# Where the blend is multiplied in: the trace products of three batches, and the division of the scores, in a fused four-layer kernel

## The chip, the cores and the metric

One Trainium2 chip, one of its cores. The metric is the device time of one launch in microseconds (us), median of the runs shown.

## The reference, cut to what matters

A batch of 16 sequences x of 256 tokens and 256 channels goes through four layers, each with a residual. The change touches the first two.

```python
# layer 0: 16 decaying traces of a gated input
h1 = gelu(x @ Wn1.T + bn1)
mod = 0.5 + sigmoid(h1 @ Wn2.T + bn2)                 # (b, t, 16)
traces = [ema(gated * mod[..., d, None], tau[d]) for d in range(16)]
blend_w = softmax(blend, axis=0)                      # (16, channels)
temporal = einsum('dbtc,dc->btc', traces, blend_w)
gate = sigmoid(temporal @ Wtemp.T + btemp)
...
# layer 1: pooling with masked softmax
p = softmax(where(mask, scores[:, None, :], -1e30), -1)
pooled = (p @ hidden) / cnt[..., None]
...
# layer 2: 8 experts and a shared one (256 -> 1024 -> 256, Silu), each with weights of its own
# layer 3: 256 -> 1024 (Gelu) -> 256, a quarter of the last weight chosen per batch
```

Here ema is the recurrence h = alpha * h + input along the tokens. Since it is linear, the blend, which is a number for each trace d and channel c, may be multiplied into the input of the trace instead of into its result: the kernel feeds gated * mod[d] * blend[d, c].

## The kernel before, in words

Channels lie on the 128 partitions, in two halves (c = 0, 1), tokens in the columns; a tile of one batch is [128, 2, 256]. Weights and activations that go into TensorE are split into a rounded high part and the rest (`rnd` on line 88, `low` on line 95), and each product is three matmuls (`mm3`, lines 101 to 103).

For each batch b, `traces` (line 247) makes the gated input, the modulation and the 16 traces, and `pooled` (line 392) makes the rest of layer 0 and the pooling. Both are generators that yield after each step. The matmul units of layer 2 (`l2_unit`, line 620: up, gate, Silu, product, split, down) and layer 3 work on pairs of batches. The driver below line 820 walks a plan of units and runs steps of `traces` and `pooled` between them, at a rate (`pace`) such that a pair's batches are ready when its units come. The units of a pair wait until `pooled` of its second batch is done: batch 0 runs alone for five experts, then pair (0, 1), and then pair (2, 3), with two pairs at a time from there. The tile scheduler afterwards orders the instructions of each engine by its own estimates, so that an order is fixed when the program is built; each engine works through its queue in order.

What the change and the steps of the prediction touch:

- Line 287 to 295: md holds 0.5 + sigmoid for 16 traces on 48 partitions. For batches 1 to 15 it is stored to a DRAM tile mdd (line 295), from which rows are loaded back, repeated on all 128 partitions.
- Lines 351 to 354: for each pair of traces (d, d+1) one load of two rows of 256 into mod, a tile [128, 2, 256] with two buffers (tag "mod", `bufs=2`); eight loads per batch on SyncE's queue.
- Lines 358 to 361: bt = ga * bl * mod, in two `scalar_tensor_tensor` of 256 columns, one for each half c, because the blend bl[:, c, d] is a number per partition and differs between the halves. ga (gp in the profile) lies in PSUM for batches 1 to 15.
- Lines 362 to 367: two scans (the recurrence) into tr, and GpSimd adds tr to the sum ta.
- Batch 0 (`fast`) has another way, lines 325 to 348: mod comes from a matmul, ScalarE scales it by bl while it copies it out (line 335), and one product of 512 columns is left (line 338).
- Lines 474 to 485: the scores of the pooling: masked minimum, exponential with its sum on ScalarE (line 477), sums times counts and reciprocal on VectorE, and then sc times that number, in two `tensor_scalar` of 256 columns on VectorE (line 485); the result is transposed on TensorE (line 493, ppt).
- Lines 549 to 556: each weight chunk of an expert is loaded raw (two buffers), rounded on ScalarE (line 88) and its rest taken on VectorE, or on GpSimd for some (line 95).

Of the kernel before, what the change touches and what calls it, by code (L numbers as in the profile page):

```python
# [8 lines left out]
F32 = mybir.dt.float32  # L9
F32R = mybir.dt.float32r  # L10
I32 = mybir.dt.int32
AF = mybir.ActivationFunctionType
ALU = mybir.AluOpType
# [4 lines left out]
S = 256  # L18
P = 128
# [9 lines left out]
STORE = 2  # L29
LAG = 2  # L30
BOOST = 400
HOLD = 3
STEPS = {"traces": 21, "pooled": 10}
FIRST = 13
# [10 lines left out]
def fused_kernel(  # L45
# [20 lines left out]
    nc = tc.nc  # L66
    V, G, A, PE = nc.vector, nc.gpsimd, nc.scalar, nc.tensor
# [3 lines left out]
    l0 = ctx.enter_context(tc.tile_pool(name="l0", bufs=1))  # L71
# [68 lines left out]
    bl = const([P, 2, ND], F32, "bl", blend)  # L140
# [106 lines left out]
    def traces(b, fast):  # L247

        xr = xin_tiles.pop(b)
        xh, xl = hl(f"x_{b}", "hA")  # L250
        rnd("v" if fast else "a", xh, xr)
        low("v" if fast else "g", xl, xr, xh)
        cx = ft("ta", f"ctx{b}")
        for c in range(2):
            last_of["cx"] = V.tensor_tensor_scan(
                cx[:, c], decay[:, ND : ND + 1].to_broadcast([P, S]), xr[:, c], 0.0, ALU.mult, ALU.add
            )
        yield
        if fast:
            split_small(O_N1, "v")  # L260
        ch, cl = hl(f"c_{b}", "hA")
        rnd("a", ch, cx)
        low("v", cl, cx, ch)

        ph = ps_l.tile([P, 512], F32, tag="ps", name=f"ph{b}")
        for k in range(2):
            o = O_N1 + k * P
            mm3(ph[:, :S], W(0, o, P), W(1, o, P), xh[:, k], xl[:, k], k == 0, k == 1)
        if fast:
            with tc.issue_after(last_of["cx"].ins):  # L270
                split_small(O_G, "v")
                split_small(O_G + 512, "v")

                V.tensor_copy(coef[:, :, NE], sgt)
                V.tensor_scalar(sgt, sgt, -1.0, 1.0, ALU.mult, ALU.add)
                V.tensor_tensor(coef[:, :, 0:NE], gat, sgt.unsqueeze(2).to_broadcast([P, NB, NE]), ALU.mult)
        hg = l0.tile([P, S], F32, tag="hg", name=f"hg{b}")
        A.activation(hg, ph[:, :S], AF.Gelu, bias=vec[:, V_BN1 : V_BN1 + 1])
        hs = l0.tile([P, S], F32R, tag="hs", name=f"hs{b}")
        rnd("a", hs, hg)  # L280
        low("v", hs[64:], hg[64:], hs[64:])
        yield
        pm = ps_l.tile([P, 512], F32, tag="ps", name=f"pm{b}")
        PE.matmul(pm[:48, :S], n2[:, 0], hs, start=True, stop=False)
        PE.matmul(pm[:48, :S], n2[:, 1], hs, start=False, stop=True)
        md = l0.tile([48, S], F32, tag="md", name=f"md{b}")
        A.activation(md, pm[:48, :S], AF.Tanh, bias=hb[:48, V_BN2 : V_BN2 + 1], scale=0.5)
        V.tensor_scalar(md, md, 0.5, 1.0, ALU.mult, ALU.add)
        if fast:
            ms = l0.tile([48, S], F32R, tag="ths", name=f"ms{b}")  # L290
            rnd("v", ms, md)
            low("v", ms[32:], md[32:], ms[32:])
        else:
            mdd = dram.tile([1, ND, S], F32, tag="mdd", name=f"mdd{b}")
            nc.sync.dma_start(mdd[0], md[0:ND])
        yield
        pg = banks(fast, f"pg{b}")

        ga = ft("ga", f"ga{b}") if fast else ps_a.tile([P, 2, S], F32, tag="ga", name=f"gp{b}")
        for m in range(2):  # L300
            for k in range(4):
                o = O_G + k * S + m * P
                xa, xb_ = (xh[:, k], xl[:, k]) if k < 2 else (ch[:, k - 2], cl[:, k - 2])
                mm3(pg(m), W(0, o, P), W(1, o, P), xa, xb_, k == 0, k == 3)
        for m in range(2):
            A.activation(ga[:, m], pg(m), AF.Tanh, bias=hb[:, V_BG + m : V_BG + m + 1], scale=0.5)
        for c in halves(fast):
            V.scalar_tensor_tensor(ga[:, c], ga[:, c], 1.0, xr[:, c], ALU.add, ALU.mult)
        yield
        sm = ft("sm", f"sm{b}")  # L310

        def soma():
            pso = ps_l.tile([P, 2, S], F32, tag="ps", name=f"pso{b}")
            for m in range(2):
                for k in range(2):
                    o = O_SO + k * S + m * P
                    mm3(pso[:, m], W(0, o, P), W(1, o, P), xh[:, k], xl[:, k], k == 0, k == 1)
            for m in range(2):
                A.activation(sm[:, m], pso[:, m], AF.Gelu, bias=vec[:, V_BSO + m : V_BSO + m + 1])

        if fast:
            split_small(O_SO, "g")
            split_small(O_TE, "g")

            tacc = ps_y.tile([P, 2, S], F32, tag="y0", name=f"ta{b}")
            for d in range(ND):
                if d % 2 == 0:
                    pb = ps_gu.tile([P, 2, S], F32, tag="gu", name=f"pb{b}_{d}")
                    for i in range(2):
                        PE.matmul(  # L330
                            pb[:, i], sel[:, d + i : d + i + 1].to_broadcast([48, P]), ms, start=True, stop=True
                        )
                mod = l0.tile([P, 2, S], F32, tag="mod", name=f"mod{b}_{d}", bufs=2)
                for c in range(2):
                    last_of["a"] = A.activation(mod[:, c], pb[:, d % 2], AF.Copy, scale=bl[:, c, d : d + 1])
                bt = ft("bt", f"bt{b}_{d}", 3)
                e = "g" if d else "v"
                last_of[e] = (V if e == "v" else G).tensor_tensor(bt, ga, mod, ALU.mult)
                tr = ft("tr", f"tr{b}_{d}", 3)
                for c in range(2):  # L340
                    V.tensor_tensor_scan(
                        tr[:, c], decay[:, d : d + 1].to_broadcast([P, S]), bt[:, c], 0.0, ALU.mult, ALU.add
                    )
                PE.matmul(tacc, ident, tr, start=d == 0, stop=d == ND - 1)
                if d == 5:
                    soma()
                if d % 2:
                    yield
        else:
            tacc = ft("ta", f"ta{b}")  # L350
            for d in range(ND):
                if d % 2 == 0:
                    mod = l0.tile([P, 2, S], F32, tag="mod", name=f"mod{b}_{d}", bufs=2)
                    nc.sync.dma_start(mod, mdd[0, d : d + 2].partition_broadcast(P))
                bt = ft("bt", f"bt{b}_{d}", 3)
                tr = tacc if d == 0 else ft("tr", f"tr{b}_{d}", 3)
                with tc.issue_after(last_of[0].ins) if b == 1 and "h" not in last_of else nullcontext():
                    for c in range(2):
                        V.scalar_tensor_tensor(
                            bt[:, c], ga[:, c], bl[:, c, d : d + 1], mod[:, d % 2], ALU.mult, ALU.mult  # L360
                        )
                for c in range(2):
                    V.tensor_tensor_scan(  # L363
                        tr[:, c], decay[:, d : d + 1].to_broadcast([P, S]), bt[:, c], 0.0, ALU.mult, ALU.add
                    )
                if d:
                    G.tensor_tensor(tacc, tacc, tr, ALU.add)  # L367
                if d == 5:
                    soma()
                yield  # L370
        th, tl = hl(f"t_{b}", "hA")
        for c in halves(fast):
            rnd("a", th[:, c], tacc[:, c])
            low("v", tl[:, c], tacc[:, c], th[:, c])
        xt = xt_tiles.pop(b)
        G.tensor_tensor(xt, xt, bet.unsqueeze(1).to_broadcast([P, 2, S]), ALU.add)
        held[b] = xt, sm, th, tl
        yield
# [13 lines left out]
    def pooled(b, fast):  # L392
# [77 lines left out]
        sc = ft("sc", f"sc{b}")  # L470
        mx = l0.tile([P, 2], F32, tag="mx", name=f"mx{b}")
        sums = l0.tile([P, 2], F32, tag="sums", name=f"sums{b}")
# [8 lines left out]
        for j in halves(fast):  # L481
            V.tensor_tensor(sums[:, j], sums[:, j], cntb[:, b, j], ALU.mult)
            V.reciprocal(sums[:, j], sums[:, j])
            for i in range(j.start, j.stop):
                V.tensor_scalar(sc[:, i], sc[:, i], sums[:, i : i + 1], None, ALU.mult)
        vh, vl = hl(f"v_{b}", "hB")
        rnd("a", vh, x1)
        low("g", vl, x1, vh)
# [248 lines left out]

    def prefetch(n, boost=BOOST):
        while n > 0 and nxt[0] < len(order):
# [101 lines left out]
    for i, item in enumerate(plan):  # L841
        kind, args, _, done = item[:4]
# [130 lines left out]
```

## Time and profile before

| what | us |
|---|---|
| median of 3 runs (lowest, highest) | 2857.16 (2855.82, 2858.89) |
| profiled execution: its time, its span | 2854.52, 2852.3 |
| TensorE matmul busy | 2781.6 (98%) |
| VectorE busy | 1442.2 (51%) |
| ScalarE busy | 1239.2 (43%) |
| GpSimd busy | 1295.4 (45%) |
| L359, the products bt, all batches | 480 x, 207.2 busy, 475 ns mean |
| L363, the scans of tr | 450 x, 285.1 busy, 672 ns mean |
| L367, GpSimd's adds into ta | 225 x, 308.4 busy, 1371 ns mean |
| L354, loads of mod | 120 x, 256 KB each, 3.5 us median to landing |

A profile is one execution. A row of its groups names the line, the engine, the operation, the tile written and the tiles read, the shape and the count; then the busy time and the mean length of one; then how long the engine had been idle just before, and whom it waited for. "L88", "L95" and "L101" to "L103" are lines of helpers that many places call, so there the tiles' names tell the place. The timeline lists an engine's instructions by start. Neighbours on an engine overlap by some 0.08 us in it, so what one costs the queue is read from start to start. A table of stages gives each engine's busy time in chosen stretches of the span.

### The profile page before, as it was taken

To read this page: it belongs to the slowest core of one execution; us is meant where nothing else is said; L and a number is where in the kernel's file an instruction comes from. 1 tells how busy PE (TensorE), PEld (TensorE's weight loads), DVE (VectorE), ACT (ScalarE), POOL (GpSimd) and SP (SyncE) were. 2 spreads that over 40 slices of the span, in tenths; PEclk is the share of its full clock that TensorE was granted. 3 is DMA by queue.
4 is the path that set the end of the run, shared out by engine and by line. 5 is a ranking of instruction groups with operands and counts; after the bars stand their busy time and mean duration, and the time that the engine had idled before them with its cause. 6 is when DMAs were issued, how large, how long until landed. Compare 5 with 4: busy or idle time off the path is not lost. (4 is left out here: it accounts for less than half of the span.)

```text
span 2852.3 us, 36958 instructions
## 1 busy us (share of the span) xinstructions
PE 2781.6 (98%) x13632; PEld 2339.8 (82%) x13632; DVE 1442.2 (51%) x2661; ACT 1239.2 (43%) x2054; POOL 1295.4 (45%) x984
## 2 busy tenths in 40 slices
PE   6889889999999999999999999999999999999999
PEld 4887778888888888888888888888888888888887
DVE  7978866665665454444544445444444542222222
ACT  5565544456444533435334443344433453233433
POOL 4755544544645453543534445344454443333333
PEclk8999999999999999999999999999999999999999
DMA  3444546547443532323433143332523242222552
GB/s 106 132 144 137 162 149 217 176 144 244 149 159 120 172 123 100 118 80 92 173 105 125 40 167 117 107 118 66 181 100 110 93 159 98 89 89 76 189 196 86
DMA packets 114694, 371.24 MB, mean 130 GB/s; under 512 B 12642, under 2 KB 30930, under 8 KB 114514
## 3 DMA queue, kind: packets, MB, share of 16 engines
q1 hardware_dynamic: 113650, 368.74, 39.0%
q8 instruction: 108, 1.77, 0.3%
q14 instruction: 72, 0.59, 0.1%
q10 hardware_dynamic: 864, 0.14, 0.0%
HBM read 304.62 MB, written 64.21 MB: 129 GB/s over the span
## 5 line engine op out<-in xcount | busy, mean ns | idle before, releaser
L95 POOL TENSOR_TENSOR hh<-h,hh 128x512 fp32r<-128x512 f32 x640 | 848.4, 1326 | 1327.1 <-ACT hh L88 1307.4
L608 DVE TENSOR_TENSOR h<-h,pu 128x512 f32<-128x512 f32 x576 | 393.9, 684 | 939.6 <-PE pu L103 818.1
L88 ACT ACTIVATE hh<-h 128x512 fp32r<-128x512 f32 x640 | 403.5, 631 | 932.6 <-DVE h L608 912.4
L101 PE MATMUL pg<-x,w_e 128*128 128x512 f32 (+1 forms) x1232 | 467.3, 379 | 12.7 <-ACT x L88 5.4
L607 ACT ACTIVATE h<-pg 128x512 f32<-128x512 f32 x576 | 342.9, 595 | 306.6 <-PE pg L103 228.5
L101 PE MATMUL pu<-x,w_e 128*128 128x512 f32 (+1 forms) x1232 | 465.4, 378 | 6.5 <-ACT h L607 3.7
L103 PE MATMUL pg<-x,w_e 128*128 128x512 f32 (+1 forms) x1232 | 465.7, 378 | 4.2 <-DVE w_e L95 3.4
L102 PE MATMUL y<-hh,w_e 128*128 128x512 f32 (+1 forms) x1232 | 464.4, 377 | 3.2 <-POOL hh L95 3.2
L102 PE MATMUL pg<-x,w_e 128*128 128x512 f32 (+1 forms) x1232 | 465.3, 378 | 0.0
L103 PE MATMUL pu<-x,w_e 128*128 128x512 f32 (+1 forms) x1232 | 463.8, 376 | 0.0
L102 PE MATMUL pu<-x,w_e 128*128 128x512 f32 (+1 forms) x1232 | 463.6, 376 | 0.0
L103 PE MATMUL y<-hh,w_e 128*128 128x512 f32 (+1 forms) x1232 | 463.5, 377 | 0.0
L101 PE MATMUL y<-hh,w_e 128*128 128x512 f32 (+1 forms) x1232 | 415.6, 377 | 1.0 <-DVE acc L655 0.8
L367 POOL TENSOR_TENSOR ta<-ta,tr 128x512 f32<-128x512 f32 x225 | 308.4, 1371 | 67.6 <-DVE tr L363 53.9
L363 DVE TENSOR_TENSOR_SCAN tr<-decay,bt 128x256 f32<-128x256 f32 x450 | 285.1, 672 | 0.0
L101 PEld LDWEIGHTS pg<-x,w_e 128*128 128x128 f32 x1232 | 232.5, 189 | 56.4 <-ACT w_e L88 6.4
L101 PEld LDWEIGHTS pu<-x,w_e 128*128 128x128 f32 x1232 | 232.1, 188 | 50.5 <-ACT h L607 5.8
L103 PEld LDWEIGHTS pg<-x,w_e 128*128 128x128 f32 x1232 | 232.7, 189 | 47.8 <-DVE w_e L95 5.2
L102 PEld LDWEIGHTS y<-hh,w_e 128*128 128x128 f32 x1232 | 233.0, 189 | 47.0 <-POOL hh L95 5.5
L101 PEld LDWEIGHTS y<-hh,w_e 128*128 128x128 f32 x1232 | 231.5, 189 | 44.8 <-ACT hh L88 1.3
L103 PEld LDWEIGHTS y<-hh,w_e 128*128 128x128 f32 x1232 | 233.0, 189 | 41.7
L103 PEld LDWEIGHTS pu<-x,w_e 128*128 128x128 f32 x1232 | 232.3, 189 | 41.9
(294 smaller groups left out, 3267.5 us busy)
## 6 DMA issues: line engine op xcount, KB each, us to landing
w_e<-keep_e SPq DMA_DIRECT2D x216, 768.0 KB, 4.4
raw_e<-in_wexp_dram SPq DMA_DIRECT2D x144, 384.0 KB, 4.5
keep_e<-w_e SPq DMA_DIRECT2D x72, 768.0 KB, 4.2
mod<-mdd SPq DMA_DIRECT2D x120, 256.0 KB, 3.5
w_f<-keep_f SPq DMA_DIRECT2D x56, 384.0 KB, 3.6
raw_c<-in_comb_dram SPq DMA_DIRECT2D x32, 260.0 KB, 2.8
xr<-in_xT_dram SPq DMA_DIRECT2D x16, 256.0 KB, 3.1
xt<-in_x_dram SPq DMA_DIRECT2D x16, 256.0 KB, 2.7
```

What stands on the lines that cost most here:

```text
L88: last_of["ca"] = A.activation(out_, in_, AF.Copy)
L95: i = (V if e == "v" else G).tensor_tensor(out_, in_, h.bitcast(F32), ALU.subtract)
L101: PE.matmul(o, wh, xh, start=start, stop=False, **kw)
L102: PE.matmul(o, wh, xl, start=False, stop=False, **kw)
L103: last_of["pe"] = PE.matmul(o, wl, xh, start=False, stop=stop, **kw)
L363: V.tensor_tensor_scan(tr[:, c], decay[:, d : d + 1].to_broadcast([P, S]), bt[:, c], 0.0, ALU.mult, ALU.add)
L367: G.tensor_tensor(tacc, tacc, tr, ALU.add)
L607: A.activation(h, ps_g, AF.Silu)
L608: last_of["h"] = V.tensor_tensor(h, h, ps_u, ALU.mult)
```

## The change

For b below `LEAN` = 4 (with the other way of batch 0: batches 1, 2 and 3) each trace has a mod tile of its own. The load repeats one row into both halves, on all partitions; ScalarE multiplies each half in place by its blend; and VectorE makes one product of 512 columns. Batches 4 to 15 keep their products. The number of mod buffers stays two. For all batches but the first, ScalarE instead of VectorE multiplies the scores by the reciprocal.

```diff
+LEAN = 4
...
             for d in range(ND):
-                if d % 2 == 0:
+                if b < LEAN:
+                    mod = l0.tile([P, 2, S], F32, tag="mod", name=f"mod{b}_{d}", bufs=2)
+                    row = mdd[0, d : d + 1].partition_broadcast(P)
+                    nc.sync.dma_start(mod, row.to_broadcast([P, 2, S]))
+                    for c in range(2):
+                        A.activation(mod[:, c], mod[:, c], AF.Copy, scale=bl[:, c, d : d + 1])
+                elif d % 2 == 0:
                     mod = l0.tile([P, 2, S], F32, tag="mod", name=f"mod{b}_{d}", bufs=2)
                     nc.sync.dma_start(mod, mdd[0, d : d + 2].partition_broadcast(P))
...
-                    for c in range(2):
+                    if b < LEAN:
+                        V.tensor_tensor(bt, ga, mod, ALU.mult)
+                    for c in range(2 if b >= LEAN else 0):
                         V.scalar_tensor_tensor(
                             bt[:, c], ga[:, c], bl[:, c, d : d + 1], mod[:, d % 2], ALU.mult, ALU.mult
                         )
...
             for i in range(j.start, j.stop):
-                V.tensor_scalar(sc[:, i], sc[:, i], sums[:, i : i + 1], None, ALU.mult)
+                if fast:
+                    V.tensor_scalar(sc[:, i], sc[:, i], sums[:, i : i + 1], None, ALU.mult)
+                else:
+                    A.activation(sc[:, i], sc[:, i], AF.Copy, scale=sums[:, i : i + 1])
```

## The prediction

> **What bounds the kernel now.** I read the page's busy shares first: TensorE (PE) is busy for 98% of the span, so over most of the kernel nothing but fewer or better-fed matmuls counts. Then the table of stages, because the change touches only batches 1 to 3 in its larger part and a share over the whole span hides them. Columns: stretch in us, its length, busy us (instructions) of PE, weight loads, VectorE (DVE), ScalarE (ACT), GpSimd (POOL), then granted clock, DMA share, GB/s.
>
> ```profile
> 76.00:126.00 50.00, 44.90 (x341) 42.76 (x339) 49.45 (x87) 24.54 (x37) 42.03 (x28) 0.97 0.46 143
> 181.00:235.00 54.00, 50.09 (x258) 41.89 (x257) 53.29 (x91) 27.97 (x42) 40.22 (x28) 0.97 0.43 129
> 268.00:322.00 54.00, 45.35 (x196) 34.44 (x195) 53.40 (x97) 23.64 (x38) 35.73 (x26) 0.97 0.36 111
> 322.00:380.00 58.00, 58.00 (x346) 51.53 (x345) 40.18 (x65) 36.72 (x64) 25.80 (x20) 1.00 0.69 227
> 380.00:396.00 16.00, 9.96 (x58) 9.01 (x57) 5.86 (x18) 4.51 (x10) 0.00 (x0) 0.79 0.17 58
> 600.00:2800.00 2200.00, 2197.68 (x10365) 1843.28 (x10364) 973.08 (x1833) 901.78 (x1492) 948.04 (x732) 1.00 0.37 124
> ```
>
> The first three stretches are the trace stages of batches 1, 2 and 3. VectorE is busy for 49.45 of 50, 53.29 of 54 and 53.40 of 54 us: it is the bound there, and PE has gaps of 5, 4 and 9 us. From 322 to 380 and from 600 on PE has none, so an engine relieved there is worth nothing. At 380 to 396 PE is nearly idle: it waits for the end of batch 3's pooled steps, because the matmul units of the pair (2, 3) can't start before. Everything up to that point decides when the saturated rest begins.
>
> Next VectorE's timeline in batch 1's stage (start us, us, engine, line, operation, tiles, count); no row has an idle time before it:
>
> ```profile
> 78.03 1.26 DVE L363 TENSOR_TENSOR_SCAN ta<-decay,bt 128x256 f32<-128x256 f32 x2
> 79.21 0.66 DVE L608 TENSOR_TENSOR h<-h,pu 128x512 f32<-128x512 f32 x1
> 79.79 1.65 DVE L359 SCALAR_TENSOR_TENSOR bt<-gp,bl,mod 128x256 f32<-128x256 f32 x4
> 81.36 0.95 DVE L95 TENSOR_TENSOR w_e<-raw_e,w_e 128x768 fp32r<-128x768 f32 x1
> 82.23 2.43 DVE L363 TENSOR_TENSOR_SCAN tr<-decay,bt 128x256 f32<-128x256 f32 x4
> ```
>
> Read it by starts, since neighbours overlap: four L359 products take 81.36 − 79.79 = 1.57, so 0.78 us for one trace's two; one 128x512 product with a PSUM operand (L608) takes 79.79 − 79.21 = 0.58 us. Last the groups that price the rest:
>
> ```profile
> L335 ACT ACTIVATE mod<-pb,bl 128x256 f32<-128x256 f32 x32 | 13.3, 472 | 5.2 <-POOL bt L338 5.1
> L485 DVE TENSOR_SCALAR sc<-sc,sums 128x256 f32<-128x256 f32 x32 | 14.1, 479 | 0.5
> ```
>
> and, from the view of the tile mod up to 330 us, how long its loads take:
>
> ```profile
> DMA to landing us min/median/max: 3.0/3.4/4.8
> ```
>
> [...] The new product reads gp from PSUM and mod from SBUF, so I price it as L608.
>
> **The change, part by part.** *Products.* 3 batches x 16 traces: 96 L359 go, 48 products of 512 columns come. 0.78 − 0.58 = 0.20 us each, 48 x 0.20 = 9.6 us, all in stretches where VectorE has no idle time. This is the ceiling. (By durations instead of starts: 40.4 us of L359 in the three stretches, less 48 x 0.66, is 8.7.)
>
> *Scaling.* 96 ACTIVATEs on ScalarE; pairs of such size (L409) take 0.84 us, so 16 x 0.84 = 13.4 us per batch, on an engine that is busy 24 to 28 of 50 to 54 us. It becomes about 38 of 47 to 51. A copy shares the table of its neighbours (in the trace the rounding copies of L88 stand between Silus without a load), so no table load is added. What is queued behind a pair of scales: the Silu of the next unit, the rounding of h, the rounding of a weight chunk. Bounds: nothing, if they fall into ScalarE's idle time (25 us per stage), and 0.84 us for each of some 9 units per stage, 8 us, if VectorE waits each time. VectorE's waits for ScalarE in batch 1's stage sum to 1.4 us today, so there is slack: I take 1.1 us in all.
>
> *Loads and buffers.* mod keeps two buffers, but a buffer now holds one trace, not two: 16 loads of 256 KB per batch instead of 8, and the load for trace d+2 can be issued only when product d has read. The SyncE queue takes 24 more issues of 0.33 us, 8 us in 170 us, which it has; but each waits for its product, and the raw loads of weight chunks stand behind it. Scaling in place also adds a wait in ScalarE's queue for the landing. The turnaround from the end of product d to product d+2 is: hop 0.1, landing, hop 0.1, scales 0.84. With the median landing of 3.4 that is 4.45 us; twice the loads and rows of 1 KB where there were 2 KB make it longer, and I take 4.1, midway to the maximum seen: 5.14 us. What VectorE leaves: products start every 2.93 us per trace in batch 1 (77.25 to 121.25 for 15), 3.07 in batch 2 (181.49 to 227.53), 3.39 in batch 3 (268.02 to 318.83); two traces less the saved 0.40 and less the product's own 0.58 are 4.89, 5.16 and 5.80 us. So batch 1 stalls 0.25 us per pair, 7.5 pairs, 1.9 of its 3.0 us; batches 2 and 3 keep their 3.0 each. Net −7.1 us. Bounds: −9 with the median landing, and above nothing with 4.8 (see the last rival).
>
> *Scores.* For batches 1 to 15 two TENSOR_SCALARs leave VectorE (0.61 us by the timeline[...]) and two ACTIVATEs of 0.84 come to ScalarE. From 600 us on PE's 2197.7 of 2200 hides both. The one exposed place is batch 3's chain at 384 us: there ScalarE is idle, so it costs 0.84 − 0.61 and a hop, 0.4 us. If a load of mod or a rounding stood ahead of it, 1 us more.
>
> *Order.* The order of the changed kernel's instructions shows the same matmuls, and the same order from the pair (2, 3) on. Ahead of that, all 56 units of the first pair still come before it, but batch 3's score product (psc) stands 16 matmuls earlier, 16 x 0.12 = 1.9 us less of the idle stretch if its inputs are there. I take half, −0.9.
>
> Sum: −7.1 + 1.1 + 0.4 − 0.9 = −6.5 us. Made against the profiled execution: 2854.5 (span 2852.3 and 2.2 around it) becomes 2848.0; the median of the runs shown stands 2.6 higher, so 2857.16 − 6.5 = 2850.7.
>
> **Rivals.** *Full relief.* The product loop never stalls and the earlier psc is fully used: −9.6 − 1.9 + 0.4 = −11.1, so 2846. For: the new order has two pairs of scans, an h product and mostly a chunk split between product d and d+2, 4.4 to 5.4 us. Against: more DMA in the same stages.
>
> *VectorE was not alone.* In batch 1's stage GpSimd is busy 42.0 of 50 us (its adds of the traces and h rests), and ScalarE waits 14.7 us there for raw weight loads. If those take over, a quarter of the gain is left: −2, so 2855. Against: GpSimd's share falls to 40.2 and 35.7 of 54 in batches 2 and 3.
>
> *The loop of two buffers becomes the bound* (slower). Landing 4.8 us, and half a chunk rounding (0.42) ahead of the scales: 0.1 + 4.8 + 0.42 + 0.1 + 0.84 = 6.26, and 0.58 for the product is 6.84 us per pair against 5.87, 6.14 and 6.78 today: (0.97 + 0.70 + 0.06) x 7.5 = 13 us, so 2870. It decides in batch 1 from a turnaround of 5.3 us (5.87 less 0.58), where the saved 0.40 is eaten. For: two buffers, three queues in the loop (SyncE, ScalarE, VectorE), each in order. Against: the median landing leaves 0.4 us of slack even in batch 1.
>
> That nothing is replaced can be excluded: the order shows 48 products of 512 columns, 96 scales and 30 divisions on ScalarE.
>
> **How the numbers follow.** Forecast 50%, full relief 20%, shared bound 17%, buffer loop 13%. The measurement of this kernel can tell about 0.2% (5.7 us) from no change. The forecast's own spread of 3 us around 2850.7 puts half of it and more beyond that line; with the full relief faster is 0.54, the rest of the forecast and the shared bound make 0.33 within it, and the loop, past its light cases, 0.13 slower. The range 2842 to 2863 takes in both bounds of the products and the lighter half of the loop's cases.
>
> **What would show it.** Right: about 48 products of 512 columns at 0.66 us under the line of the product, no idle time of VectorE before them, stages of 48, 51 and 51 us, and the first matmul of the pair (2, 3) some 6 us earlier, with the rest unchanged. Wrong: VectorE idle before the products until ScalarE's mod, and ScalarE idle before the scales until the load of mod; or stages as long as before with GpSimd at 95%. Outside all this: the rest after 400 us changing its own length.

## The result, and the profile after

| | before | after |
|---|---|---|
| median of 5 runs on one chip, us (lowest, highest) | 2855.82 (2853.93, 2858.89) | 2899.07 (2897.22, 2901.5) |
| span of the profiled execution, us | 2852.3 | 2898.4 |

The ratio is 1.0151, with a 95% interval of 1.014 to 1.0162: the change makes the kernel 43 us slower. In this document "+43" always means ratio less 1, times 2855, against runs of the kernel before on the same chip. The time lies outside the range, on the side to which 0.13 had been given.

The table of stages after, in the same stretches, with one more for the gap ahead of the pair (2, 3), which now lies 46.4 us later (columns as above: PE, PEld, VectorE, ScalarE, GpSimd, granted clock, DMA share, GB/s):

```profile
76.00:126.00 50.00, 42.64 (x302) 41.44 (x303) 39.74 (x56) 30.52 (x53) 29.71 (x21) 0.88 0.54 148
181.00:235.00 54.00, 40.60 (x244) 37.04 (x243) 32.10 (x48) 32.97 (x59) 21.76 (x14) 0.84 0.55 137
268.00:322.00 54.00, 48.81 (x231) 39.30 (x229) 38.86 (x57) 29.65 (x53) 25.31 (x17) 0.97 0.40 115
426.40:442.40 16.00, 11.14 (x74) 10.13 (x72) 5.30 (x17) 5.58 (x12) 1.29 (x1) 0.89 0.19 58
600.00:2800.00 2200.00, 2198.00 (x10422) 1844.49 (x10421) 983.06 (x1845) 919.04 (x1530) 956.17 (x738) 1.00 0.37 125
```

From 600 on PE still has no gap worth counting (2198.00 of 2200). The stages have moved: batch 2's products now start at 211.0 and batch 3's at 309.1, so the second and third stretch no longer hold the same work as before. VectorE was full in all three and is not any more (39.74 of 50, 32.10 and 38.86 of 54), yet in the first two PE does less as well (42.64 where it was 44.90, 40.60 where it was 50.09): everybody waits. The first score product of batch 3 (psc), which opens the last step ahead of the pair (2, 3), starts at 381.7 before:

```profile
L467 PE MATMUL psc<-ths,vr x1: 280/280/280, 381.7 to 381.7; 128*128 128x256 f32 x1
```

and at 428.1 after:

```profile
L476 PE MATMUL psc<-ths,vr x1: 280/280/280, 428.1 to 428.1; 128*128 128x256 f32 x1
```

So the whole loss, 46.4 us in these two executions, is made by then. The view of the tile mod from 60 to 460 us shows its place (numbers of a row: shortest, median, longest ns, first and last start; below, the idle time of an engine just ahead of an instruction on mod, by what it waited for):

```profile
L358 ACT ACTIVATE mod<-mod,bl x96: 491/497/514, 72.0 to 366.0; 128x256 f32<-128x256 f32 x96
L356 SPq DMA_DIRECT2D mod<-mdd x48: 359/377/491, 65.3 to 360.3; - x48
L366 DVE TENSOR_TENSOR bt<-gp,mod x48: 657/684/693, 85.2 to 367.8; 128x512 f32<-128x512 f32 x48
its engine sat idle before it (us, times) until:
  DMA mod<-mdd: 71.5, 36
  ACT mod L358: 14.5, 16
...
DMA to landing us min/median/max: 3.3/5.3/9.1
```

The new instructions last what they should (684 ns, 497 ns). But a load lands after 5.3 us, where it took 3.4; ScalarE stands idle for it 36 times, 71.5 us in all, and VectorE waits only 14.5 us for ScalarE. The prediction had named this picture among its signs of being wrong; the stall that it priced on VectorE sits mainly one engine earlier. What that does is seen at the start of batch 2's stage, in ScalarE's timeline:

```profile
188.47 0.82 ACT L89 ACTIVATE w_e<-raw_e 128x768 fp32r<-128x768 f32 x1
193.19 0.51 ACT L358 ACTIVATE mod<-mod,bl 128x256 f32<-128x256 f32 x1 [3.90 <-DMA mod<-mdd]
193.61 0.61 ACT L89 ACTIVATE hh<-h 128x512 fp32r<-128x512 f32 x1
194.12 0.49 ACT L358 ACTIVATE mod<-mod,bl 128x256 f32<-128x256 f32 x1
195.97 0.91 ACT L358 ACTIVATE mod<-mod,bl 128x256 f32<-128x256 f32 x2 [1.35 <-DMA mod<-mdd]
196.79 0.89 ACT L497 ACTIVATE sc<-sc,sums 128x256 f32<-128x256 f32 x2
197.70 1.28 ACT L619 ACT_TABLE_LOAD   x1
198.99 0.60 ACT L619 ACTIVATE h<-pg 128x512 f32<-128x512 f32 x1
```

and, of the same stretch, in TensorE's:

```profile
189.81 0.28 PE L103 MATMUL pu<-x,w_e 128*128 128x256 f32 x1
194.27 0.79 PE L102 MATMUL y<-hh,w_e 128*128 128x256 f32 x2 [4.18 <-ACT hh L89]
194.87 0.41 PE L104 MATMUL pg<-x,w_e 128*128 128x256 f32 x1
195.08 0.41 PE L102 MATMUL pg<-x,w_e 128*128 128x256 f32 x1
```

ScalarE's next instruction is the scaling of a trace that nobody needs yet (batch 2's first product starts at 211.0); its load isn't there; behind it in the queue stands the rounding of h (hh), for which PE's next matmul waits 4.18 us. Its h has been there since 187.25 (VectorE's last product of it starts at 186.57 and takes 0.68), but it starts at 193.61, after the scaling: here the queue was worked through in order. Then come a second wait for a load, the division of the scores and the Silu. This repeats; the view of waits from 60 to 460 us (us in total, times, longest):

```profile
POOL hh L96 <- ACT hh L89: 111.8, 43, 10.6
ACT mod L358 <- DMA mod<-mdd: 71.5, 36, 6.2
PE y L102 <- ACT hh L89: 13.6, 8, 4.2
PE pu L102 <- ACT h L619: 11.7, 8, 4.6
```

Before, the same view has GpSimd's wait for hh at 88.2 us and PE's wait for Silu (h) at 3.7, and no matmul of y waiting for hh from ScalarE at all (only weight loads for y do, 1.0 us in 4 times).

This wait costs PE twice. After it the granted clock is low: between 189.8 and 194.2 PE has almost no work, and in the next 4.8 us the clock is 0.50 (columns as in the table of stages; the third row is a little later):

```profile
189.80:194.20 4.40, 0.29 (x3) 0.08 (x1) 0.56 (x2) 1.01 (x3) 0.00 (x0) 0.80 0.89 205
194.20:199.00 4.80, 4.73 (x22) 4.73 (x23) 0.00 (x0) 3.42 (x8) 1.28 (x1) 0.50 0.30 110
203.00:206.00 3.00, 3.00 (x16) 3.00 (x16) 0.79 (x3) 0.98 (x2) 1.17 (x1) 0.50 0.64 198
```

The matmuls above start 0.21 us apart (194.87, 195.08), not 0.12 as at 189.69 and 189.81. So 4.8 us at a clock of 0.50 follow a gap of 4.2 us. What sets the clock is not shown: the third row is at 0.50 too, and the two gaps shortly before it, ended by the matmuls at 200.37 and 201.90, were under 0.8 us each (0.77 and 0.79). The length of the last gap alone does not tell the clock here. The shares come from the time up to psc, before:

```profile
0.00:381.70 381.70, 329.18 (x1862) 275.26 (x1863) 310.50 (x551) 213.89 (x363) 221.29 (x161) 0.96 0.45 140
```

and after:

```profile
0.00:428.10 428.10, 348.07 (x1847) 292.00 (x1848) 311.21 (x498) 253.75 (x463) 220.22 (x161) 0.90 0.50 140
```

PE's idle time rises from 52.5 to 80.0 us, by 27.5. Its matmul time rises from 329.2 to 348.1 us, by 18.9, although some 15 matmuls fewer now stand ahead of psc; the mean granted clock falls from 0.96 to 0.90. Together 46.4: about three fifths of the loss are waits, two fifths the longer matmuls at the lower clock. (A few matmul records may be missing.)

### The profile page after: what moved, and what is told of

Its sections match the earlier page's. It is cut to its first block, busy times and chain, and to the rows that moved or that the text cites. A ratio compares the mean times of both kernels' runs of the same rounds, so it can differ in the third digit from the quotient of the medians.

```text
span 2898.4 us, 37115 instructions
## 1 busy us (share of the span) xinstructions
PE 2801.7 (97%) x13632; PEld 2356.6 (81%) x13632; DVE 1433.5 (49%) x2583; ACT 1289.3 (44%) x2180; POOL 1292.5 (45%) x984
## 5 line engine op out<-in xcount | busy, mean ns | idle before, releaser
L102 PEld LDWEIGHTS pg<-x,w_e 128*128 128x128 f32 x1232 | 235.4, 191 | 61.7 <-ACT x L89 11.6
L102 PEld LDWEIGHTS y<-hh,w_e 128*128 128x128 f32 x1232 | 232.2, 190 | 61.4 <-ACT hh L89 16.4
L102 PEld LDWEIGHTS pu<-x,w_e 128*128 128x128 f32 x1232 | 235.1, 191 | 56.8 <-ACT h L619 16.2
L103 PEld LDWEIGHTS y<-hh,w_e 128*128 128x128 f32 x1232 | 234.1, 190 | 46.9 <-POOL hh L96 5.5
L104 PEld LDWEIGHTS pu<-x,w_e 128*128 128x128 f32 x1232 | 235.5, 191 | 42.3
L103 PEld LDWEIGHTS pu<-x,w_e 128*128 128x128 f32 x1232 | 235.2, 191 | 41.1
```

The costliest lines, as they stand in the source:

```text
L102: PE.matmul(o, wh, xh, start=start, stop=False, **kw)
L103: PE.matmul(o, wh, xl, start=False, stop=False, **kw)
L104: last_of["pe"] = PE.matmul(o, wl, xh, start=False, stop=stop, **kw)
```

## The experiments

The theory formed from this trace, called Queue: the loss is ScalarE's wait at the head of its in-order queue for late loads, and what stands behind. The rival, Work: it is the 13 us of added ScalarE work per batch, wherever it waits. In the diffs "-" is the change and "+" the experiment, unless the text says that it starts from the kernel before.

**One part alone.** Products and scaling without the scores (line 497 on VectorE for all batches):

```diff
-                if fast:
-                    V.tensor_scalar(sc[:, i], sc[:, i], sums[:, i : i + 1], None, ALU.mult)
-                else:
-                    A.activation(sc[:, i], sc[:, i], AF.Copy, scale=sums[:, i : i + 1])
+                V.tensor_scalar(sc[:, i], sc[:, i], sums[:, i : i + 1], None, ALU.mult)
```

> The products of the change, with the scores divided on VectorE as before. Queue theory (ScalarE waits in its in-order queue for late loads of mod, and what stands behind waits too): nearly all of the 43 us stay, 30 to 43 us slower than before, since the scores are behind such a wait only once, in batch 1's pooled steps, where the trace has a 9.3 us wait. Scores theory (the division on ScalarE is what delays the chain): at most 15 us slower than before remain.

Measured: 2890.79 us, ratio 1.0127 (1.011 to 1.0144), +36.

The scores alone (the kernel before with the four "-" lines above in the place of the "+" line):

> Only the division of the scores moves to ScalarE; traces and loads as before. Queue theory: no load of mod stands in ScalarE's queue, so within 3 us of before. Scores theory: 20 us slower or more.

Measured: 2858.47, ratio 1.001 (1.0001 to 1.0019), +3. The scores are the small part.

The change's loads alone: VectorE keeps its two products with the blend, ScalarE scales nothing, the scores stay on VectorE.

```diff
-                    for c in range(2):
-                        A.activation(mod[:, c], mod[:, c], AF.Copy, scale=bl[:, c, d : d + 1])
...
-                    if b < LEAN:
-                        V.tensor_tensor(bt, ga, mod, ALU.mult)
-                    for c in range(2 if b >= LEAN else 0):
+                    for c in range(2):
                         V.scalar_tensor_tensor(
-                            bt[:, c], ga[:, c], bl[:, c, d : d + 1], mod[:, d % 2], ALU.mult, ALU.mult
+                            bt[:, c], ga[:, c], bl[:, c, d : d + 1], mod[:, c if b < LEAN else d % 2], ALU.mult, ALU.mult
```

> The loads of the change (one row repeated into both halves, one trace per buffer, two buffers) for batches 1 to 3, but VectorE keeps its two products with the blend, and the scores stay on VectorE. So ScalarE neither scales nor waits for mod. Queue theory: VectorE now waits for the loads where ScalarE did; without ScalarE in the loop only a part of the loss is left, 5 to 20 us slower than before. Work theory (the 96 scalings fill ScalarE): same as before within 3 us. Loads theory (the loads are late, and whoever waits for them loses the same): 35 us slower or more.

Measured: 2868.02, ratio 1.0044 (1.0028 to 1.0061), +13:

```profile
  DMA mod<-mdd: 8.4, 10
DMA to landing us min/median/max: 3.0/5.0/8.3
```

The same loads, landing after 5.0 us, cost a third of the loss where VectorE is the one that waits for them (8.4 us in all). That fits Queue, since ScalarE's queue then runs on; but this run also leaves out the scaling, so by itself it does not part the wait from the work. The next run does that from the other side.

The old loads (two traces each, two buffers, so four traces deep); ScalarE writes the scaled row into bt and VectorE multiplies in bt:

```diff
-                if b < LEAN:
-                    mod = l0.tile([P, 2, S], F32, tag="mod", name=f"mod{b}_{d}", bufs=2)
-                    row = mdd[0, d : d + 1].partition_broadcast(P)
-                    nc.sync.dma_start(mod, row.to_broadcast([P, 2, S]))
-                    for c in range(2):
-                        A.activation(mod[:, c], mod[:, c], AF.Copy, scale=bl[:, c, d : d + 1])
-                elif d % 2 == 0:
+                if d % 2 == 0:
...
                 bt = ft("bt", f"bt{b}_{d}", 3)
+                if b < LEAN:
+                    for c in range(2):
+                        A.activation(bt[:, c], mod[:, d % 2], AF.Copy, scale=bl[:, c, d : d + 1])
...
-                        V.tensor_tensor(bt, ga, mod, ALU.mult)
+                        V.tensor_tensor(bt, ga, bt, ALU.mult)
```

> The change, but with the loads of before (two traces per load, two buffers, so up to four traces ahead); ScalarE writes the scaled row into bt, and VectorE multiplies bt by ga in place. Same instructions on ScalarE and VectorE as the change, scores on ScalarE. Queue theory: the loads are there before ScalarE comes to them, so the loss goes: within 5 us of before, or up to 8 us faster by the shorter products. Work theory: still 30 us slower or more than before.

Measured: 2862.76, ratio 1.0026 (1.0016 to 1.0036), +7. The same work on ScalarE with other loads and buffers: five sixths of the loss are gone, so Work can't be the main cause. But the gain does not come back either. The same with the scores on VectorE:

> The kernel before with only the scaling moved to ScalarE (into bt, from the old loads of two traces, four traces deep); scores divided on VectorE as before. Queue theory (what costs is ScalarE's wait at the head of its queue): with the late loads gone and without the scores, 3 to 6 us over before. Work theory (13.4 us more of ScalarE per batch is what costs): 5 to 8 over, about the same as with the scores moved. Relief as once predicted: 3 to 8 us under before.

Measured: 2865.57, ratio 1.0037 (1.0023 to 1.0051), +11. Above what Queue expected (3 to 6), and above Work's 5 to 8 too. Its interval (+7 to +15) overlaps that of the run above (+5 to +10), so whether taking the scores back gains or costs anything here can't be told. That a few us go with the order of the instructions, which each edit changes, is a guess.

**What of the loads costs: depth, rows or the hold.** From the run with the old loads, one load of one row per trace, into one half of the tile:

```diff
-                if d % 2 == 0:
+                if b < LEAN:
+                    mod = l0.tile([P, 2, S], F32, tag="mod", name=f"mod{b}_{d}", bufs=2)
+                    nc.sync.dma_start(mod[:, d % 2], mdd[0, d].partition_broadcast(P))
+                elif d % 2 == 0:
```

> As the run with the old loads (scaled row written into bt), but each load brings one trace's row once (128 KB in rows of 1 KB), into two buffers: depth of two traces as in the change, half of its bytes. If the depth of two traces makes the loss, +20 to +40 over before, with a landing of about 3.5 to 4.5 us and ScalarE's wait for the loads above 40 us. If the doubled bytes and packets make it, within 5 us of the run with the old loads (+3 to +12), with ScalarE's wait below 20 us.

Measured: 2861.49, ratio 1.0022 (1.0014 to 1.0029), +6, with a landing of 3.3 us and 12.6 us of ScalarE's waits for loads. A depth of two traces is not what costs, though the run with the old loads alone could be read so.

The change, with each row stored twice in DRAM, so that a load has 128 rows of 2 KB instead of 256 of 1 KB:

```diff
-            mdd = dram.tile([1, ND, S], F32, tag="mdd", name=f"mdd{b}")
-            nc.sync.dma_start(mdd[0], md[0:ND])
+            if b < LEAN:
+                mdd = dram.tile([1, ND, 2, S], F32, tag="mdt", name=f"mdt{b}")
+                for i in range(2):
+                    nc.sync.dma_start(mdd[0, :, i], md[0:ND])
+            else:
+                mdd = dram.tile([1, ND, S], F32, tag="mdd", name=f"mdd{b}")
+                nc.sync.dma_start(mdd[0], md[0:ND])
...
-                    row = mdd[0, d : d + 1].partition_broadcast(P)
-                    nc.sync.dma_start(mod, row.to_broadcast([P, 2, S]))
+                    nc.sync.dma_start(mod, mdd[0, d].partition_broadcast(P))
```

> The change with the row of mdd stored twice in DRAM, so that a load of 256 KB has 128 rows of 2 KB instead of 256 of 1 KB; depth two traces as in the change. If the short rows make the landing of 5.3 us and the loss with it, landing 3.4 to 4 us and at most +25 over before. If the depth is what counts, landing may fall to 4 to 5 us, and +33 to +45 stays.

Measured: 2873.33, ratio 1.0061 (1.0044 to 1.0078), +17. Of its view of mod, 60 to 460 us:

```profile
L360 SPq DMA_DIRECT2D mod<-mdt x48: 319/327/1058, 64.2 to 330.8; - x48
  DMA mod<-mdt: 39.5, 21
DMA to landing us min/median/max: 3.0/3.7/6.5
```

The change's own loads, but scaled into bt (the scaling edit of the old-loads run, with mod[:, c] for its source):

> The change with its loads (256 rows of 1 KB, two buffers), but ScalarE writes the scaled row into bt and VectorE multiplies in bt, so a buffer of mod is free again when ScalarE has read it and no longer when VectorE's product has. If holding the buffer until the product is what makes the late loads cost, the time falls to +15 to +27 over before, with a landing still of 5 us or more. If the landing itself is the cost, +33 to +45 as in the change.

Measured: 2882.19, ratio 1.0092 (1.0074 to 1.011), +26:

```profile
  DMA mod<-mdd: 46.4, 22
DMA to landing us min/median/max: 3.0/5.1/7.7
```

Both at once, 128 rows of 2 KB and into bt:

> The change's loads of 256 KB with the depth of two traces, but as 128 rows of 2 KB, and scaled into bt, so that the buffer is free when ScalarE has read it. If the number of packets makes the late landing: +5 to +12 over before, near the one-row loads (128 packets, 128 KB) at +6, with a landing of 3.7 us or less. If the bytes make it: +20 to +30, near the run into bt with 256 packets at +27.

Measured: 2858.37, ratio 1.0012 (1.0005 to 1.0019), +3, somewhat under what was expected:

```profile
L360 SPq DMA_DIRECT2D mod<-mdt x48: 319/327/433, 62.6 to 310.9; - x48
  DMA mod<-mdt: 14.6, 11
  DVE tr L377: 11.8, 15
DMA to landing us min/median/max: 3.0/3.5/5.4
```

These four make a square, all with two buffers, 256 KB per load and the scores on ScalarE:

| | scaled in place, held until the product | scaled into bt, free when ScalarE has read |
|---|---|---|
| 256 rows of 1 KB | +43 (ScalarE waits 71.5 us for loads) | +26 (46.4) |
| 128 rows of 2 KB | +17 (39.5) | +3 (14.6) |

The 256 short rows cost 26 or 23 us, the hold 17 or 14, each known to some 5 us, and the two add almost without a rest. What is left of the change beside them is +3.

This, with the scores on VectorE:

> The run with 128 rows of 2 KB into bt, with the scores divided on VectorE as before. If the division on ScalarE costs its own 3 us here as it did alone: +0 to +1 over before. If it is a matter of no change once the stage has slack: +2 to +5, as with it.

Measured: 2855.72, ratio 1.0002 (0.9993 to 1.0011): no difference from before that can be told. It is the best version with the whole computation, and no faster than the kernel before. Its ScalarE still waits for loads, more than in the run just before it:

```profile
  DMA mod<-mdt: 20.0, 11
```

So waits of this size need not leave the kernel slower.

**Where the gain went.** From the kernel before, VectorE's relief alone. One product of 512 columns, the row of mod repeated by a stride of zero, no blend:

```diff
-                    for c in range(2):
+                    if b < 4:
+                        V.tensor_tensor(bt, ga, mod[:, d % 2].unsqueeze(1).to_broadcast([P, 2, S]), ALU.mult)
+                    for c in range(2 if not (b < 4) else 0):
                         V.scalar_tensor_tensor(
```

> The kernel before with VectorE's relief alone: for batches 1 to 3 one product of 512 columns per trace, with the row of mod repeated by a stride of zero; loads, depth and ScalarE as before. The blend is left out of the computation. If VectorE alone was the bound of the three stages, 7 to 11 us under before. If others take over at once (ScalarE, GpSimd, TensorE's own wait for roundings), within 3 us of before.

Measured: 2850.21, ratio 0.9981 (0.9974 to 0.9988), -5. The two trace stages of batches 2 and 3 in its table:

```profile
181.00:235.00 54.00, 47.46 (x248) 40.75 (x248) 49.54 (x73) 25.88 (x39) 35.05 (x25) 0.93 0.43 134
268.00:322.00 54.00, 50.64 (x230) 41.56 (x230) 52.34 (x85) 26.59 (x44) 41.30 (x28) 0.97 0.40 124
```

So the ceiling of 9.6 was never there: relief for nothing is worth 3 to 7 us, about half of it. Which engine takes over, these runs don't show; VectorE itself is still busy for 49.54 and 52.34 of 54 us.

From the kernel before, 96 scalings on ScalarE of a scratch tile, read and written by nothing else:

```diff
+    scr = l0.tile([P, S], F32, name="scr")
+    nc.gpsimd.memset(scr, 1.0)
...
+                if b < 4:
+                    for c in range(2):
+                        A.activation(scr, scr, AF.Copy, scale=bl[:, c, d : d + 1])
```

> The kernel before, with 96 extra ScalarE scalings of 128x256 beside the products of batches 1 to 3, on a scratch tile that nothing else reads or writes: the change's added work on ScalarE with no wait for a load, a buffer or a product. The output is that of the kernel before. Work theory: +8 us or more over before. Queue theory: within 4 us of before, and no more than 6 us more of waits for ScalarE's roundings on PE.

Measured: 2862.15, ratio 1.0023 (1.0014 to 1.0033), +7. And both, the relief and these scalings:

> The relief without the blend and the 96 scales on a scratch tile, in one kernel: VectorE's relief and ScalarE's added work together, with no wait between the two. The blend is left out of the computation. If the parts add: -5.4 + 6.8 = +1.4, so within 4 us of before, and what the run with the old loads has above this is its waits for bt and mod. If the work costs more once VectorE is relieved: +6 to +10.

Measured: 2851.16, ratio 0.9992 (0.9985 to 0.9999), -2. Neither run prices what it was made for: since the scratch tile waits for nothing, the scheduler put all 96 ahead of the stages of batches 2 and 3 (view of the tile scr in the first of them):

```profile
L359 ACT ACTIVATE scr<-scr,bl x96: 491/507/550, 12.3 to 119.0; 128x256 f32<-128x256 f32 x96
```

Hence two more, in which the scalings read the loaded row, which puts them beside the products:

```diff
-                        A.activation(scr, scr, AF.Copy, scale=bl[:, c, d : d + 1])
+                        A.activation(scr, mod[:, d % 2], AF.Copy, scale=bl[:, c, d : d + 1])
```

> The kernel before, with 96 extra scalings on ScalarE that read the loaded row of mod (old loads, depth of four traces) and write a scratch tile that nothing reads: the change's added work at its place in ScalarE's queue. VectorE keeps its two products, and the output is that of the kernel before. If the added work at this place is what is left of the cost: +6 to +10. If it is hidden by ScalarE's idle time, as the prediction had it: within 3 us of before.

Measured, beside the kernel before's products: 2865.51, ratio 1.0033 (1.002 to 1.0045), +9.

> The same 96 scalings beside VectorE's relief without the blend (one product of 512 columns from the old loads). The blend is left out of the computation. If the parts add, the run above less 5.4 us: near +2. If the relief is given back in full to ScalarE's queue: +4 to +8, near the runs with old loads into bt. If ScalarE's work is hidden: -5 to -3, and what the runs into bt have above that are their waits for bt.

Measured, beside the relief: 2864.32, ratio 1.0029 (1.0019 to 1.004), +8. In the view of scr's source mod of the run without relief:

```profile
L359 ACT ACTIVATE scr<-mod,bl x96: 492/508/513, 68.3 to 320.7; 128x256 f32<-128x256 f32 x96
...
  DMA mod<-mdd: 21.2, 14
```

At its place the scaling is not hidden (+9, between 6 and 13). Even with the old loads, landing after 3.4 us, ScalarE reaches it before the row is there 14 times and idles 21.2 us. That these waits make the +9 is not shown: the best version above has 20.0 us of them and stands at +1. Beside this work the relief gives 1 us in place of 5, but the intervals of the two runs are too wide to tell these apart.

**One batch alone.** The change's trace had been read as if batch 3's stage ended no later than it began, so it seemed free of loss. The change for b == 3 only (the test is replaced wherever it stands), scores on VectorE:

```diff
-LEAN = 4
+LEAN = 3
...
-                if b < LEAN:
+                if b == LEAN:
```

> The change for batch 3 alone (its loads, scaling in place, one product), batches 1 and 2 and the scores as before. From the change's trace, where batches 1 and 2 lose about 23 us each and batch 3 ends no later than it began: within 4 us of before. If each stage loses alike under the late loads, +12 us.

Measured: 2864.52, ratio 1.0037 (1.0024 to 1.0051), +11. That reading was wrong. By their first score products, batch 1 is 21.9 us late in the change (183.8 against 161.9), batch 2 39.4 (367.8 against 328.4) and batch 3 46.4: the third stage adds 7.0. The one-row loads into bt, for batch 3 only:

> As the run with one-row loads into bt, but for batch 3 alone, with the scores on VectorE as before. If ScalarE's added work costs about 2 us per batch (a third of the run with the scales alone) and VectorE's relief is worth its 3 us in this stage: within 3 us of before, perhaps 1 to 3 under. If the relief is worth nothing, +2.

Measured: 2857.77, ratio 1.0009 (1.0002 to 1.0016), +3.

## Why the prediction was wrong, point by point

**What bounds the kernel** was read rightly in its frame: all of the loss falls ahead of the pair (2, 3), none from 600 on. (Only "nearly idle" is too strong for PE from 380 to 396: its row has 9.96 busy of 16.) What failed is what was built on it: that ScalarE's 25 us of idle time per stage would cover new work that waits for loads.

**Products, -9.6 at most, -7.1 taken.** The durations held (684 ns for the new one; L608, as which it was priced, had a mean of 684 before). The size did not: the relief alone gives 5. The second rival, VectorE not alone, was nearer in kind, since part of the gain is lost without any new wait; it had put a quarter of it left, and about half is.

**Scaling, +1.1: the first failed step.** It was set against ScalarE's idle time. The instruction was priced well (497 ns; 0.91 us for a pair where 0.84 was taken), its place was not. No table load came with it (100 before and 100 after, 48 of each ahead of the Silus of layer 2). The prediction named the right neighbours in the queue (Silu, the roundings) and bounded their delay by the length of a pair, 0.84 us. That bound counts no wait. This one waits for a load, and what stands behind it is delayed by the wait, up to 6.2 us in the change. With the old loads, at its place beside VectorE's two products, the scaling measured +9 (6 to 13), some 8 times the sum's term; how much of that is waiting stays open. Products and scaling together, -6.0 in the sum, come to +1 in the best version.

**Loads and buffers: the second failed step, and the larger.** "I take 4.1, midway to the maximum seen": the median is 5.3, above the maximum that the old loads showed (4.8). The load was priced from one of another shape, the same 256 KB in half as many rows, though the text itself noted the shorter rows; as many loads of 256 KB in rows of 2 KB landed after 3.5 to 3.8. The turnaround then is 0.1 + 5.3 + 0.1 + 0.84 = 6.34 us (the hops of 0.1 are the prediction's; the first product of batch 1 ends at 85.90, and the next load is issued at 85.93), past the 5.3 from which the loop decides; with 0.58 for the product it makes 6.92 us per pair. Products of batches 1, 2 and 3 run from 85.2 to 140.8, 211.0 to 270.5 and 309.1 to 367.8, by the view of mod cut into three stretches:

```profile
L366 DVE TENSOR_TENSOR bt<-gp,mod x16: 666/684/692, 85.2 to 140.8; 128x512 f32<-128x512 f32 x16
L366 DVE TENSOR_TENSOR bt<-gp,mod x16: 675/690/692, 211.0 to 270.5; 128x512 f32<-128x512 f32 x16
L366 DVE TENSOR_TENSOR bt<-gp,mod x16: 657/680/693, 309.1 to 367.8; 128x512 f32<-128x512 f32 x16
```

That is 7.4, 7.9 and 7.8 us per pair of traces, where 5.87, 6.14 and 6.78 stood before and where the slower rival, the loop of two buffers, had put 6.84; what stretches the pairs beyond 6.92 is not taken apart here. So this rival named the right loop, the right engines and the right point, and gave 13 us where these stretches are longer by 11.6, 13.5 and 7.9, 33 in all. Its term counted VectorE's stall only. The prediction did write that "scaling in place also adds a wait in ScalarE's queue for the landing", and put no price on it. That is the term that was missing: 71.5 us of waits in the queue on which PE, VectorE and GpSimd wait, and on PE a granted clock of 0.50 after the wait shown above. With short rows and hold mended, all but 3 us of the loss are gone.

The rest to the 46.4 us: batch 1's products start 8.0 later (85.2 against 77.25), of which 5.3 are seen in ScalarE's queue, where the first scalings stand ahead of the roundings of q, batch 0's last step (q at 74.92 where it was 69.62); between batches 1 and 2 another 10.0 go (70.2 against 60.2); after the ends of batches 2 and 3 it is 1.9 and 2.6 less. 33.0 + 8.0 + 10.0 - 1.9 - 2.6 = 46.5. ScalarE's timeline at the start of batch 1's stage:

```profile
72.02 0.91 ACT L358 ACTIVATE mod<-mod,bl 128x256 f32<-128x256 f32 x2 [5.89 <-DMA mod<-mdd]
73.75 0.91 ACT L358 ACTIVATE mod<-mod,bl 128x256 f32<-128x256 f32 x2 [0.82 <-DMA mod<-mdd]
74.56 0.42 ACT L307 ACTIVATE gp<-pg,hb 128x256 f32<-128x256 f32 x1
74.92 0.37 ACT L89 ACTIVATE q<-ppt0g 128x256 fp32r<-128x256 f32 x1
```

Of batch 3's 7.9, 4.5 are made up around it. Alone, with batches 1 and 2 undisturbed, the same stage costs +11 (7 to 15). Whether the losses of the three stages add, these runs don't show: three times 11 is not far from the +36 of the change without the scores.

**Scores, +0.4.** +3 alone; 7 less when it is taken out of the change (43 to 36), 3 less out of the best of the square (3 to 1) and 3 more out of the run with the old loads (7 to 11), both within the noise. Alone, 0.4 is not excluded either (+0.3 to +5); in the change the bound given, 1 us more if a load of mod stands ahead, was too small. In ScalarE's timeline at the start of batch 2's stage the division stands behind such a load, and the Silu behind the division.

**Order, -0.9.** Not tried by itself. Some 15 matmuls fewer do stand ahead of psc (1847 where it was 1862). The gap ahead of the pair has 4.9 us without a matmul in 16 (426.4 to 442.4), where it was 6.0; the 1.9 us hoped for are at most 1.1.

**What is left open.** The runs with the scaling on ScalarE and sound loads lie between +1 and +11 (into bt, 256 KB in long rows; into bt, old loads; scratch). Their loads land after 3.3 to 3.6 us and their scalings last the same. ScalarE's waits for loads don't order them: 20.0 us in the run at +1, 7.0 in the one with the old loads at +7 (each in its one profiled execution). In these profiles psc starts at 385.4 in the run at +1 and at 394.1 in the one at +7. Whether waits for bt or another order of instructions is behind that, these runs don't tell. Nor was it tried to shift the scaling itself behind the roundings in ScalarE's queue.

## What to carry to other kernels

Before giving a half-idle engine more work, ask whether the new instruction can find its input missing: where a queue is worked through in order, as here, a wait delays everything that is queued behind it, and the idle time shown is no cover for that. Price a changed transfer by a row of its own shape, in number of rows as in bytes, and count how long its buffer is held and by whom. Where TensorE is the bottleneck, count the lower clock with its waits: here 27.5 us of added idle time came with 19 us of longer matmuls (mean granted clock 0.90 where it was 0.96).

## What the runs showed of the hardware that was not expected

- Loads of mod, onto 128 partitions: 256 rows of 1 KB land after 5.0 to 5.3 us (medians of four kernels; where batch 3 alone has them, 16 of them and 8 of the old loads together after 4.6), 128 rows of 2 KB, the same bytes, after 3.5 to 3.8 in three kernels, and 128 rows of 1 KB after 3.3 in one. In these kernels twice the rows for the same bytes took 1.2 to 1.8 us longer, and half the bytes in as many rows 0.2 to 0.5 less. The issue on SyncE takes 366 to 377 ns against 326 or 327 and 323.
- A gap of 4.2 us on PE was followed by 4.8 us of work at a granted clock of 0.50, and a later stretch of 3 us at 0.50 followed two gaps of under 0.8 us (0.77 and 0.79). Longer matmuls made 19 of the 46 us lost.
